# Adjacency transpositions ahead of the node tiles' stages in the hooks between passes

## The chip, the cores and the metric

The kernel runs on one core of a Trainium2 chip (trn2). Times are microseconds (us) of device time of one execution. The core has a matrix engine (TensorE, "PE", with its weight loads shown as "PEld"), a vector engine (VectorE, "DVE"), a scalar engine (ScalarE, "ACT"), GpSimd ("POOL") and a queue engine that issues DMAs (SyncE, "SP"). Each runs its own instructions in the order in which they were laid out.

## The reference

Four graph layers work on 3327 nodes with 512 features and one dense 0/1 adjacency `adj` (3327 x 3327, int32). Layers 0 to 2 are graph attention with 8, 4 and 8 heads, layer 3 is a mean over neighbours followed by a dense layer:

```python
h = jnp.maximum(_layernorm(x, axis=-1), 0.0)
# attention layer (0; layers 1 and 2 alike)
Wh = jnp.einsum('nd,hdo->hno', h, W)
e = jax.nn.leaky_relu(f1[:, :, None] + f2[:, None, :], negative_slope=0.2)   # f1, f2: Wh . a1, Wh . a2
e = jnp.where(adj[None, :, :] > 0, e, NEG_INF)
h_prime = jnp.einsum('hnm,hmo->hno', jax.nn.softmax(e, axis=-1), Wh)
x = x + elu(h_prime)
# layer 3
agg = mask @ h / jnp.maximum(deg, 1.0)
x = x + relu(concat([h @ W_self + b_self, agg @ W_nb + b_nb]) @ W_comb + b_comb)
```

## The kernel before

The nodes are cut into 26 tiles of 128 rows (the last has 127). Output rows are worked in seven *chunks*: six of four tiles and one of two. Neighbour tiles are gathered in five *groups* of 6, 6, 6, 4 and 4 tiles (`JG`).

**Attention.** For every chunk and head, the loop in `attention` builds two 0/1-like matrices per group (`tht`, `gt`: comparisons on ACT, L652, and on DVE, L649, then a bitwise "and" and "xor" with the transposed mask, L656 and L658). Then come *passes*: in layer 0 a pass is two row tiles times 26 neighbour tiles times two matmuls (L748 and L751), 104 matmuls in all, accumulated in two PSUM buffers `acc`. DVE reduces the result (L766) and later steps normalise it.

**Hooks.** After every pass `hooks.run` is called once. A hook emits a little of two other kinds of work, so that it runs between the passes:

- *Node stages.* When a chunk of layer l is done, its rows go on to layer l+1, tile by tile, one stage per hook. Every third hook takes up a new tile. Stage 0 is `finish`: load the tile's x rows (SP), two activations (L848, L849, ACT), a combination (L850, DVE), an addition on POOL (L851) and its store, issued by POOL (L852). Then follow the statistics of the normalisation (L330 and L334 on DVE, L335 to L337 on POOL), the normalised rows (L342, ACT), their transposition on PE (L138, four 128 x 128 blocks into a PSUM tile `tp`, copied out by ACT at L142), the projection (L398, 16 matmuls in layer 0's attention), scaling (L429, L432, L435), splitting into pieces (L372 on DVE, L376 and L382 on ACT, L364 and L380 on POOL) and stores (SP; also L500, a small transposition, and L503 once per chunk).
- *Mask steps.* In layer 0 the adjacency is transposed. One piece is one row tile and one group: 130 pieces. A piece is loaded by a DMA that POOL issues (L226, tile `at`, int32 to bf16, three buffers), turned by PE (L234, one 128 x 128 transposition per neighbour tile, into a PSUM tile `tp`), made into a mask by DVE (L238; for pieces on the diagonal also L241 and L242) and stored by SP (L243). Pieces at an edge first have a DVE memset (L223, L225). One mask step turns piece i-1 and then loads piece i. A hook of chunk 0 runs one or two steps in turn; a hook of a later chunk runs two in every third hook and one else. The 130 pieces end in chunk 4 of layer 0; after that the list of mask steps is empty.

Both L138 and L234, and the small transpositions, share two PSUM buffers of the name `tp`.

Before the attention of layer 0 there is a *node phase* that projects all 26 tiles of layer 0. It is a loop over the same `hooks.run`, with no pass between two hooks; from its third turn on each hook also runs one mask step (21 of them, for 20 pieces).

In layer 0's chunk 0 (layer 0 has no finished chunk yet) the hooks have no node stages, only mask steps and, from head 3 on, one of eight folds of the next layer's weights (L316 and L320, DVE).

**Order.** The framework lays out each engine's instructions; it need not keep the order in which the code emits them, but it keeps data dependences and the orders that `after` states. `after(inst, name)` puts an instruction behind another in that order, and makes no wait on the chip. The load and the first transposition of a mask step, and the first operation of most node stages, are put behind `gone[-1]`, the last matmul of the pass that has just been emitted:

```python
ld = nc.gpsimd.dma_start(at[:n, :w], adj[t * P:t * P + n, j0 * P:j0 * P + w])
after(ld, gone[-1] if gone else stored[NT - 1] if c else relus[-3])
```

The load of x rows in layer 0's `finish` stands behind the first pass only (`gone[0]`), and L848 to L852 have no such order.

Of the kernel before, what the change touches and what calls it, by code (L numbers as in the profile page):

```python
# [52 lines left out]
def tile_gnn(ctx: ExitStack, tc: tile.TileContext, x, adj, W0, a01, W1, al, ar, W2, a2,  # L53
# [197 lines left out]
    def mask_tiles(c, self_loops=False):  # L251
        t0, nt = chunks[c]
        tiles, loops = [], []
        for g, (j0, nj) in enumerate(JG):
            v = mask_view(c, g)
            nc.sync.dma_start(v, maskd[c][g])
            if self_loops:
                for k in range(nt):
                    if j0 <= t0 + k < j0 + nj:
                        loops.append((v[:, k, t0 + k - j0, :].bitcast(U32), dg1[:, t0 + k, :].bitcast(U32)))  # L260
            tiles.append(v)
        if self_loops != "later":
            set_loops(loops)
        return (tiles, loops) if self_loops == "later" else tiles
# [328 lines left out]
    class Hooks:  # L593
# [3 lines left out]
            self.masks, self.tiles, self.flying, self.small, self.done = [], [], [], [], 0  # L597

        def run(self, every, n, masks=1, steps=1):
            for st in list(self.flying):  # L600
                for _ in range(min(steps, len(st))):
                    st.pop(0)()
                if not st:
                    self.flying.remove(st)
            if self.small:
                self.small.pop(0)()
            if self.tiles and n % every == 0:
                st = self.tiles.pop(0)
                st.pop(0)()
                self.flying.append(st)  # L610
            for _ in range(masks):
                if self.masks:
                    self.masks.pop(0)()

        def drain(self):
            while self.tiles or self.flying:
# [20 lines left out]
    def matrices(L, nt, h, g, s1v, mask, pt, gt):  # L637


        l = L.l  # L640
        j0, nj = JG[g]
        gv, pv = [t[:, :nt * nj * P].rearrange("p (k j i) -> p k j i", k=nt, j=nj) for t in (gt, pt)]
        gu, pu = [t[:, :nt * nj * P].bitcast(U32) for t in (gt, pt)]
        mu = mask.rearrange("p k j i -> p (k j i)").bitcast(U32)

        def compare(jj):
            j = j0 + jj
            if j in GP_ON_DVE[l]:
                nc.vector.tensor_scalar(gv[:, :, jj, :], s1v, L.ns2[:, j, h:h + 1], 2.0,  # L649
                                        op0=ALU.is_gt, op1=ALU.mult, saturate=False)  # L650
            else:
                nc.scalar.activation(gv[:, :, jj, :], s1v, AF.Relu, bias=L.ks2[:, j, h:h + 1], scale=BIG,  # L652
                                     saturate=False)

        def split():
            nc.vector.tensor_tensor(pu, gu, mu, ALU.bitwise_and)  # L656
            if l != 1:
                nc.vector.tensor_tensor(gu, pu, mu, ALU.bitwise_xor)  # L658
        return pv, gv, (pu, mu), [lambda jj=jj: compare(jj) for jj in range(nj)] + [split]
# [219 lines left out]
    with tc.tile_pool(name="first", bufs=1) as fp:  # L879
# [30 lines left out]
        while hooks.tiles or hooks.flying:  # L910
# [4 lines left out]
            for g in range(3):  # L915
                if n == (8, 15, 21)[g]:
# [7 lines left out]
                    pv, gv, _, steps = matrices(L, PER, 0, g, early["s1"], masks0[g], b[:, :s], b[:, s:2 * s])  # L924
# [41 lines left out]
    with tc.tile_pool(name="agg", bufs=1, reuse_waits="tile") as op:  # L966
# [21 lines left out]
        for c, (t0, nt) in enumerate(chunks):  # L988
            masks = m0 if c == 0 else mask_tiles(c)
# [476 lines left out]
```

## Time and profile before

| | us |
|---|---|
| median of 3 runs | 3612.37 |
| lowest and highest | 3606.46, 3613.09 |
| the profiled execution, its own time | 3606.74 |
| its span in the profile | 3605.0 |
| first transposition L234 starts, last one ends | 37.2, 1012 |

| group of instructions | number | busy us | mean ns |
|---|---|---|---|
| L748 and L751, matmuls of the passes (PE), each | 10744 | 1838 | 249 |
| L234, transpositions of adjacency (PE) | 676 | 60.0 | 221 |
| L238, masks out of PSUM (DVE) | 110 + 20 | 91.9 + 16.9 | 844 |
| L226, loads of adjacency, issue on POOL | 130 | 73.7 | 568 |
| L851, additions of `finish` (POOL) | 72 | 124.6 | 1730 |
| L852, their stores, issue on POOL | 72 | 46.6 | 647 |
| L138, transpositions of node tiles (PE) | 416 | 64.5 | 279 |
| L142, their copies (ACT) | 108 | 62.0 | 576 |

Matmuls overlap in the array, so a mean of 249 ns goes with a distance of some 84 ns between two of them. "Idle before" and the list of waits name what an engine waited for last; idle time of an engine other than the one that bounds a stretch costs nothing. The view by stretch gives, for each stretch, its length, the busy time and number of instructions of PE, PEld, DVE, ACT and POOL, the granted share of PE's clock, the busy share of the DMA engines and GB/s.

### The profile page before, as it was taken

How to read it: one execution, taken by the hardware profiler on the slowest of the kernel's cores; microseconds unless marked ns; L12 is line 12 of the kernel's file. 1: busy time of each engine (PE TensorE's matmuls, PEld its weight loads, DVE VectorE, ACT ScalarE, POOL GpSimd, SP SyncE). 2: the span in 40 equal slices, each digit the busy share in tenths (PEclk: the TensorE clock that was granted, in tenths of full speed). 3: DMA queues.
4: the chain of work that ended last, by engine and by line, in shares of the span. 5: the costliest groups of instructions: out<-in, count | busy, mean ns of one | idle time of the engine just before them, and what ended most of it. 6: DMA issues, size and time to landing. Idle time of an engine off the chain costs nothing. (4 is left out here: it accounts for less than half of the span.)

```text
span 3605.0 us, 78609 instructions
## 1 busy us (share of the span) xinstructions
PE 3480.3 (97%) x31323; PEld 3143.9 (87%) x31323; DVE 2660.0 (74%) x5227; ACT 2512.7 (70%) x4113; POOL 633.4 (18%) x858
## 2 busy tenths in 40 slices
PE   7899999999999899999999989999999999999999
PEld 6799999999999878888888869989898989876887
DVE  8798887878887779898888868877676767672221
ACT  5777787777787888888888767766676667572111
POOL 6601221111110211232323230001010101020000
PEclk9999999999999999999999999999999999999999
DMA  7787786777766878777777876655555555576431
GB/s 219 226 239 204 205 235 195 214 206 214 223 203 205 294 261 295 263 271 280 273 255 275 296 286 214 200 168 174 179 194 178 175 177 184 166 262 250 128 97 61
DMA packets 321384, 779.00 MB, mean 216 GB/s; under 512 B 36233, under 2 KB 145108, under 8 KB 320368
## 3 DMA queue, kind: packets, MB, share of 16 engines
q1 hardware_dynamic: 287154, 704.38, 58.1%
q0 software_dynamic: 28128, 62.42, 7.4%
q10 hardware_dynamic: 5726, 7.08, 0.6%
q8 instruction: 249, 4.08, 0.4%
q14 instruction: 127, 1.04, 0.1%
HBM read 663.59 MB, written 129.64 MB: 220 GB/s over the span
## 5 line engine op out<-in xcount | busy, mean ns | idle before, releaser
L751 PE MATMUL acc<-ab,gt 128*128 128x195 bf16 (+1 forms) x10744 | 1837.8, 249 | 8.2 <-DVE rc L788 3.7
L748 PE MATMUL acc<-ab,tht 128*128 128x195 bf16 (+1 forms) x10744 | 1838.2, 249 | 6.9 <-DVE tht L656 6.0
L652 ACT ACTIVATE gt<-s1b,ks 128x512 fp8e4<-128x512 f32 (+1 forms) x2448 | 1449.8, 680 | 337.9 <-PE acc L751 204.8
L751 PEld LDWEIGHTS <-gt 128*128 128x128 fp8e4 x10744 | 1055.4, 98 | 28.6 <-issue 19.4
L748 PEld LDWEIGHTS <-tht 128*128 128x128 fp8e4 x10744 | 1055.4, 98 | 19.8 <-DVE tht L656 7.3
L656 DVE TENSOR_TENSOR tht<-gt,m 128x768 uint32<-128x768 uint32 (+3 forms) x557 | 445.4, 800 | 133.0 <-ACT gt L652 130.9
L658 DVE TENSOR_TENSOR gt<-tht,m 128x768 uint32<-128x768 uint32 (+3 forms) x557 | 449.3, 807 | 8.7
L649 DVE TENSOR_SCALAR gt<-s1b,ns 128x512 fp8e4<-128x512 f32 (+1 forms) x446 | 221.7, 501 | 161.8 <-PE acc L751 158.8
L741 PE MATMUL acc<-ab,ts 128*128 128x258 f32 x2496 | 333.4, 289 | 6.2 <-ACT ts L624 3.4
L624 ACT CAST ts<-tht 128x1536 fp32r<-128x1536 fp8e4 x208 | 300.3, 1472 | 54.6 <-PE acc L741 51.3
L741 PEld LDWEIGHTS acc<-ab,ts 128*128 128x128 f32 x2496 | 313.3, 190 | 14.7 <-issue 3.8
L1002 PE MATMUL acc<-y,mf 128*128 128x512 f32 x1352 | 311.4, 392 | 2.3 <-DVE mf L997 2.3
L652 ACT ACTIVATE tht<-s1b,ks 128x512 fp8e4<-128x512 f32 (+1 forms) x504 | 308.9, 683 | 3.3 <-DMA s1b<-s 2.8
L1002 PEld LDWEIGHTS acc<-y,mf 128*128 128x128 f32 x1352 | 254.7, 188 | 58.8 <-DVE mf L997 2.7
L766 DVE TENSOR_REDUCE R<-acc 128x130 f32<-128x390 f32 x416 | 214.8, 557 | 100.6 <-PE acc L751 99.9
L851 POOL TENSOR_TENSOR xt<-xt,e 128x512 f32<-128x512 f32 x72 | 124.6, 1730 | 913.2 <-DVE e L850 588.1
L744 PE MATMUL acc<-ab,tht 128*128 128x387 bf16 x1248 | 225.8, 329 | 7.0 <-DMA ab<-ab 3.8
L999 ACT CAST mf<-m 128x768 fp32r<-128x768 fp8e4 (+1 forms) x78 | 59.2, 763 | 247.2 <-PE acc L1002 235.4
L741 PE MATMUL acc<-ab,tv 128*128 128x258 f32 x1664 | 218.7, 283 | 0.9 <-DMA ab<-ab 0.4
L741 PEld LDWEIGHTS acc<-ab,tv 128*128 128x128 f32 x1664 | 207.1, 189 | 2.5 <-DVE tv L624 1.0
L398 PE MATMUL mm<-w,hT 128*128 128x260 f32 (+1 forms) x832 | 197.0, 391 | 8.5 <-DVE AB L435 5.1
L380 POOL TENSOR_TENSOR pt<-r 128x520 bf16<-128x520 f32 (+1 forms) x116 | 136.6, 1198 | 318.0 <-DVE r L372 301.1
(160 smaller groups left out, 3516.3 us busy)
## 6 DMA issues: line engine op xcount, KB each, us to landing
ab<-ab SPq DMA_DIRECT2D x333, 600.0 KB, 5.4
ab<-ab SPq DMA_DIRECT2D x222, 400.0 KB, 4.0
ab<-ab SPq DMA_DIRECT2D x112, 774.0 KB, 6.2
ab<-ab SPq DMA_DIRECT2D x112, 516.0 KB, 5.7
ab<-ab SPq DMA_DIRECT2D x56, 582.0 KB, 6.0
s1b<-s SPq DMA_DIRECT2D x120, 256.0 KB, 5.9
m<-mask SPq DMA_DIRECT2D x69, 384.0 KB, 4.0
ab<-pt SPq DMA_DIRECT2D x13, 1600.0 KB, 7.2
```

The lines of the kernel that those rows point to most:

```text
L398: mm = nc.tensor.matmul(pw[:, o:e], hT[:, k, :], L.w[:, k, f, o:e], start=(k == 0), stop=(k == KC - 1))
L624: (nc.scalar.copy if KIND[g] == "s" else nc.vector.tensor_copy)(t[:, :k1 - k0, :nj], th[a][g][:, k0:k1])
L649: nc.vector.tensor_scalar(gv[:, :, jj, :], s1v, L.ns2[:, j, h:h + 1], 2.0, op0=ALU.is_gt, op1=ALU.mult, saturate=False)
L652: nc.scalar.activation(gv[:, :, jj, :], s1v, AF.Relu, bias=L.ks2[:, j, h:h + 1], scale=BIG, saturate=False)
L656: nc.vector.tensor_tensor(pu, gu, mu, ALU.bitwise_and)
L658: nc.vector.tensor_tensor(gu, pu, mu, ALU.bitwise_xor)
L741: mm = nc.tensor.matmul(acc[k][:, :2 * DA], thr[g][:, k - ks[0], jj, :], ab[a][g][:, jj, :], start=(j == 0), stop=(j == NT - 1), skip_grou ...
L744: mm = nc.tensor.matmul(acc[k][:, :3 * DA], th[a][g][:, k, jj, :], ab[a][g][:, jj, :3 * DA], start=(j == 0), stop=(j == NT - 1), skip_grou ...
L748: nc.tensor.matmul(acc[k][:, :3 * DA + o], th[0][g][:, k, jj, :], ab[0][g][:, jj, :3 * DA + o], start=(j == 0), stop=False, skip_group_che ...
L751: mm = nc.tensor.matmul(acc[k][:, AO:AO + 3 * DA + o], th[1][g][:, k, jj, :], ab[0][g][:, jj, AO:AO + 3 * DA + o], start=False, stop=(j == ...
L766: nc.vector.tensor_reduce(R[:, k], v.rearrange("p a (s d) -> p a d s", s=3), AX.X, ALU.add)
L1002: nc.tensor.matmul(acc[k], mf[:, jj, :], y2[g][:, jj, s, :], start=(j0 + jj == 0 and s == 0), stop=(j0 + jj == NT - 1 and s == 1))
```

## The change

The two lines that run the mask steps move from the end of `Hooks.run` to its beginning. In every hook the mask steps are now emitted ahead of the running node tiles' stages, of the fold, and of the first stage of a new tile. Nothing else is changed; the operations, their number and their data are the same. Where a mask step looks up `gone[-1]` it finds the same matmul as before; in the node phase `relus[-3]` is read before the hook adds a tile's activation to the list, so it names that of the tile before.

```diff
         def run(self, every, n, masks=1, steps=1):
+            for _ in range(masks):
+                if self.masks:
+                    self.masks.pop(0)()
             for st in list(self.flying):
                 for _ in range(min(steps, len(st))):
                     st.pop(0)()
...
                 st = self.tiles.pop(0)
                 st.pop(0)()
                 self.flying.append(st)
-            for _ in range(masks):
-                if self.masks:
-                    self.masks.pop(0)()
```

## Prediction

> **What bounds the kernel now.** I read the page first. TensorE (PE) is busy for 97% of the span, every other engine for 74% or less, so work moved about on the others costs nothing until it makes PE wait. Adjacency is transposed only up to 1012 us (line L234 below), so only that part is affected directly; I asked for busy time by stretch: node phase of layer 0, then its row chunk 0, then its chunks 1 to 4, where the last transposition runs.
>
> ```profile
> PE 3480.3 (97%) x31323; PEld 3143.9 (87%) x31323; DVE 2660.0 (74%) x5227; ACT 2512.7 (70%) x4113; POOL 633.4 (18%) x858
> ```
> ```profile
> 0.00:160.00 160.00, 127.20 (x640) 105.63 (x641) 128.01 (x241) 103.57 (x218) 111.03 (x181) 0.94 0.75 216
> 160.00:329.00 169.00, 164.97 (x1921) 162.38 (x1920) 148.79 (x298) 132.47 (x220) 20.97 (x35) 0.98 0.80 237
> 329.00:1013.00 684.00, 653.86 (x7336) 640.44 (x7334) 555.67 (x1090) 512.76 (x865) 120.79 (x185) 0.98 0.75 212
> ```
>
> The columns are length, then busy PE, PEld, DVE, ACT, POOL. The third stretch leaves PE idle for 30.1 us. The list of waits and the view of tile `at` say on what, and how long a load takes to land:
>
> ```profile
> PE tp L234 <- DMA at<-in_adj_dram: 30.6, 11, 5.1
> ```
> ```profile
> L234 PE MATMUL tp<-identb,at x676: 216/219/314, 37.2 to 1012.1; 128*128 128x128 bf16 x169
> ...
> DMA to landing us min/median/max: 2.9/4.8/10.2
> ```
>
> Two of the 11 waits (1.1 us) are in chunk 0; nine, 29.5 us, are at hooks of chunks 1 to 4 that run two mask steps ("double hooks"): the second step transposes a tile whose load the first step issued in the same hook. One of them, on PE and on POOL:
>
> ```profile
> 394.94 0.60 PE L138 MATMUL tp<-ident,h 128*128 128x128 f32 x4
> 395.37 0.50 PE L234 MATMUL tp<-identb,at 128*128 128x128 bf16 x6
> ...
> 399.48 0.51 PE L234 MATMUL tp<-identb,at 128*128 128x128 bf16 x6 [2.18 <-DMA at<-in_adj_dram]
> ```
> ```profile
> 392.59 1.82 POOL L851 TENSOR_TENSOR xt<-xt,e 128x512 f32<-128x512 f32 x1 [14.48 <-DMA xt<-in_x_dram]
> 394.71 0.58 POOL L852 DMA_DIRECT2D x<-xt  x1 [0.30 <-POOL xt L851]
> 395.29 1.07 POOL L226 DMA_DIRECT2D at<-in_adj_dram  x2
> ```
>
> POOL works in order. A node tile's addition L851 waited 14.48 us for its x rows, and the loads of `at` stood behind it and the store L852; the load issued at 395.29 landed at 399.44 and PE stood until then. Where POOL was free the load went out far ahead and PE did not wait. A long wait also costs afterwards: after the 4.47 us wait ending at 335.52 the matmuls come 0.16 us apart instead of 0.08 until 341.1. By the length of the passes (16.6 us there, 9.2 to 9.4 in a like hook without a wait) the nine waits cost some 41 us.
>
> **What the Trainium skill says.** "DMA: Bandwidth & Descriptors", section "SWDGE vs HWDGE vs iDMA": a DMA that converts its type is issued from GpSimd alone; here all 130 loads of `at` (int32 to bf16) are POOL's. The same page, "Anatomy of one DMA", fits 2.0 us + bytes/436e3 us; 128 x 768 int32 (393 KB) gives 2.9 us, this trace's minimum, against a median of 4.8 us: the measured figures are used. "TensorE: Matmul & The Clock Gate", Part 1, has the array drop to half rate after about 3.4 us idle and need about as long to return; the trace agrees on the halving, but takes 5.3 us to return.
>
> **The change, part by part.** No instruction, wait or byte is added or removed; in each hook the mask steps are emitted ahead of the node stages. Emission is not the order of execution: the second L234 of a double hook sits inside the next pass, and at 333.07 us POOL runs L851 of a tile emitted three hooks later. The emission order acts as a priority among instructions ready together. What moves with a mask step: on POOL the load L226 (0.54 us of issue), on DVE a memset of `at` in tiles at an edge (L225, 0.06 us; L223, 0.38), L238 (0.84) and for 26 tiles the diagonal's L241 and L242 (0.59), on PE L234, on SP the store L243 (0.3).
>
> *Node phase.* Hooks follow each other with no pass between, so stages-masks-stages-masks becomes masks-stages-masks-stages: the same ring, with the 20 masks one hook (about 5 us) earlier. One transposition (PE 6 x 0.08 = 0.5 us, DVE L238 0.95 us) leaves the tail and joins the head, near 30 us, where DVE is continuously busy. Gain at most 1.5 us; cost at most the same plus one early load, 393 KB at the page's 216 GB/s = 1.8 us, among the first x rows. Between -1.5 and +3.3, taken as 0.
>
> *Chunk 0.* There are no node stages, only eight weight folds (DVE 0.69 + 0.68 us) in hooks 8 to 15, which fall behind an L238 of 0.84 us. No PE wait there hangs on either: 0, at most 1 us if a fold becomes late for layer 1; it has over 50 us.
>
> *Hooks with a projection* (one per node tile, 16). L398 takes 3.5 us and then came L234; now L234 is first, needing its `at` 3.5 us earlier. I took each tile's landing from the trace: the tightest of the 16 is the turn at 613.60, landed 609.67, 3.9 us before. Still 0.4 us in hand; cost 0, at worst 1 us. If that cover goes, PE stands with L398 behind it.
>
> *Double hooks with a node transposition* (16). L234 (0.4 to 0.5 us) now precedes L138, whose copy L142 on ACT moves back as much. The second L234 takes the PSUM buffer which L142 frees. L142 ended 0.1 us ahead of that L234 at 365.7, 0.2 ahead at 708.3 and 879.3, about 1 us ahead in most others; in the four at 431, 602, 779 and 951 ACT was late for other reasons and PE already waits 0.13 to 0.22. Moving it 0.45 costs 0.2 to 0.4 us in some three hooks: +1 us, between 0 and 4. DVE's L238 comes earlier, and L372 or L435 behind it up to 0.95 us later, one pass ahead of their need: 0.
>
> *POOL and SP.* Both loads of a hook now rank ahead of its L851 and L852. But a load is ordered behind the pass's last matmul, and L851 is not, so it can still be placed first. In all 23 double hooks from 329 us the second L234 stands 1.9 to 2.2 us behind the pass's end, before any wait, whether the run had one or not: the order was laid out with POOL free at that point, L851 and L852 already past. They were late only on the chip. So the ranking changes nothing in most; where L851 ended after the pass did (331 us, perhaps 739 and 917), L852 may fall behind the load, 0.58 + 0.30 us each. Gain 0 to 3 us, taken as 1. On SP the mask store L243 moves with its L238, ahead of node stores; x rows (SP) are ordered by free buffers: 0, within 1.
>
> The sum: +1 - 1 = 0. The profiled execution took 3606.74 us (span 3605.0 and 1.7 around it), 5.6 under the median 3612.37; on the scale of the median I predict 3612.
>
> **Rivals.** *The loads overtake (faster).* If the ranking does put the load ahead of L851 where PE waited, up to 41 us go: 3571 if in all nine, 3592 in half, 3605 if only L852 is overtaken in eight (8 x 0.88). For: POOL's order above is the cause of the waits. Against: the even 2 us, and the ordering behind the last matmul. *The PSUM buffer (slower).* If the second L234 gets the buffer of the first, freed by L238 on DVE instead of L142, it waits for L238: in the trace L238 ends after that L234's start by 0.05 to 3.0 us in 12 of the 16 double hooks with L138, 14.0 us together, and DVE, 81% busy in this stretch, evicts the pass first. Less what the earlier L234 saves, about 10 to 14: 3624. It decides where L142 is laid out later than L238. For: L142's place on ACT was already the limit in four hooks. Against: L142 ended 0.8 to 4.1 us ahead of L238 in 13 of the 16. *It does nothing:* if ties are few, the engines' order is hardly altered: 3612, on the forecast's side. A further spread comes from a layout that shifts by tenths of a us and so makes or removes a 4 to 7 us wait at another of the 23 hooks.
>
> **How the numbers follow.** 0.2% is 7.2 us, about what a measurement of this kernel can tell. No change in balance has 0.50 (its own range 3605 to 3619); slower 0.32, the buffer or two new DMA waits of 7 us, 3620 to 3630; faster 0.18, waits lost at two or more hooks, 3571 to 3604. For 8 in 10 the range takes in the buffer rival and two waits lost: 3596 to 3630.
>
> **What would show it.** Right: the first stretch stays within 3 us of 160; L234 precedes L138 and L398 on PE; nine or so waits of L234 on `at` remain, near 30 us; POOL still has L851 ahead of L226 at 395. Waits of L234 on DVE L238 mean the buffer rival; L226 ahead of L851 and PE idle in the third stretch under 15 us mean the faster one; a change after 1013 us, or in the node phase by over 5 us, means that I looked in the wrong place.

## Result and the profile after

| | before | after |
|---|---|---|
| median (us) | 3610.75 | 3611.93 |
| lowest and highest | 3600.95, 3614.79 | 3605.49, 3623.74 |
| executions | 12 | 12 |
| the profiled execution, its own time and span | 3606.74, 3605.0 | 3614.18, 3612.4 |

The ratio after to before is 1.0009, with a 95% interval from 0.9998 to 1.002. That is no change in time, and 3611.93 lies beside the predicted 3612. The profiled execution of after happens to be 7.4 us longer than that of before; executions of one and the same kernel lie up to 18 us apart, so that difference says nothing by itself. The two profiles are used here for where PE waits.

The first line is from the page of after (busy time of each engine), the next three are its view by stretch (length, busy PE, PEld, DVE, ACT, POOL, granted clock, DMA share, GB/s):

```profile
PE 3484.3 (96%) x31323; PEld 3144.2 (87%) x31323; DVE 2656.3 (74%) x5227; ACT 2510.3 (69%) x4113; POOL 622.8 (17%) x858
```
```profile
0.00:160.00 160.00, 126.15 (x643) 104.44 (x644) 124.25 (x241) 102.57 (x217) 111.44 (x181) 0.95 0.74 216
160.00:329.00 169.00, 163.75 (x1927) 161.44 (x1926) 149.34 (x298) 132.84 (x221) 21.43 (x35) 0.99 0.79 237
329.00:1013.00 684.00, 653.42 (x7308) 639.03 (x7306) 554.72 (x1087) 510.47 (x862) 120.28 (x185) 0.98 0.74 212
```

The same number of instructions runs, and in the third stretch (chunks 1 to 4) PE is busy for 653.42 us instead of 653.86. On the total alone the change does nothing. The list of waits of PE, cut to 329 to 1013 us, says otherwise (us in total, times, longest), first of before, then of after:

```profile
PE tp L234 <- DMA at<-in_adj_dram: 29.5, 9, 5.1
PE tp L234 <- ACT hT L142: 0.4, 2, 0.2
```
```profile
PE tp L234 <- DMA at<-in_adj_dram: 24.7, 9, 4.5
PE tp L138 <- DVE st L238: 3.4, 4, 1.6
PE tp L500 <- DVE st L238: 1.2, 1, 1.2
PE tp L138 <- DVE d L241: 0.8, 1, 0.8
PE tp L138 <- ACT pt L382: 0.4, 1, 0.4
```

So the load waits lost 4.8 us, and 5.8 us of another kind of wait came in: the node transpositions L138 and L500, which are not in the list of before, now wait for a PSUM buffer `tp`, which, but for 0.4 us, is DVE's to empty. **Two effects of 5 us cancel.**

The hook that the prediction showed is still as it was on POOL:

```profile
391.36 1.88 POOL L851 TENSOR_TENSOR xt<-xt,e 128x512 f32<-128x512 f32 x1 [13.80 <-DMA xt<-in_x_dram]
393.53 0.58 POOL L852 DMA_DIRECT2D x<-xt  x1 [0.30 <-POOL xt L851]
394.11 1.07 POOL L226 DMA_DIRECT2D at<-in_adj_dram  x2
```

On PE it has a new order:

```profile
393.75 0.50 PE L234 MATMUL tp<-identb,at 128*128 128x128 bf16 x6
...
399.59 0.51 PE L234 MATMUL tp<-identb,at 128*128 128x128 bf16 x6 [3.49 <-DMA at<-in_adj_dram]
400.52 0.79 PE L138 MATMUL tp<-ident,h 128*128 128x128 f32 x4
```

L851 still waits for its x rows, ahead of the load, and PE still waits for the load (3.49 us here, 2.18 before). But L138 did not land between the two L234, where the prediction had put it: it stands behind both. Here that costs nothing, because the first L234's buffer was emptied while PE stood for the load (L238 ended at 398.6). In a double hook whose load is on time it does cost. The same hook of before (first fence, PE timeline) and of after (second fence: PE, then DVE):

```profile
460.39 0.60 PE L138 MATMUL tp<-ident,h 128*128 128x128 f32 x4
460.83 0.39 PE L234 MATMUL tp<-identb,at 128*128 128x128 bf16 x4
...
462.57 0.50 PE L234 MATMUL tp<-identb,at 128*128 128x128 bf16 x6
```
```profile
462.55 0.39 PE L234 MATMUL tp<-identb,at 128*128 128x128 bf16 x4
...
464.71 0.50 PE L234 MATMUL tp<-identb,at 128*128 128x128 bf16 x6
...
466.85 0.63 PE L138 MATMUL tp<-ident,h 128*128 128x128 f32 x4 [1.56 <-DVE st L238]
```
```profile
463.94 1.23 DVE L372 TENSOR_TENSOR r<-AB 128x1032 f32<-128x1032 f32 x1
465.08 1.03 DVE L766 TENSOR_REDUCE R<-acc 128x130 f32<-128x390 f32 x2
466.03 1.54 DVE L238 TENSOR_SCALAR st<-tp 128x512 fp8e4<-128x512 bf16 x2
```

There are two `tp` buffers and three users in this hook. Before, the third user was the second L234, and the first to come free was the buffer of L138, which ACT's L142 (0.6 us) had emptied by 461.6. After, both L234 come first and the third user is L138. Both buffers are then DVE's to empty, and DVE does L372 and L766 first: L238 starts at 466.03, 3.1 us behind the end of the first L234, and L138 stands for 1.56 us.

### The profile page after: what moved, and what is told of

The parts are those of the page before. It is cut to its first block, busy times and chain, and to the rows that moved or that the text cites. A ratio compares the mean times of both kernels' runs of the same rounds, so it can differ in the third digit from the quotient of the medians.

```text
span 3612.4 us, 78611 instructions
## 1 busy us (share of the span) xinstructions
PE 3484.3 (96%) x31323; PEld 3144.2 (87%) x31323; DVE 2656.3 (74%) x5227; ACT 2510.3 (69%) x4113; POOL 622.8 (17%) x858
## 3 DMA queue, kind: packets, MB, share of 16 engines
q14 instruction: 128, 1.05, 0.1%
## 5 line engine op out<-in xcount | busy, mean ns | idle before, releaser
L748 PEld LDWEIGHTS <-tht 128*128 128x128 fp8e4 x10744 | 1054.6, 98 | 21.6 <-DVE tht L656 8.2
L766 DVE TENSOR_REDUCE R<-acc 128x130 f32<-128x390 f32 x416 | 214.7, 556 | 100.1 <-PE acc L751 99.5
L851 POOL TENSOR_TENSOR xt<-xt,e 128x512 f32<-128x512 f32 x72 | 124.0, 1722 | 920.5 <-DVE e L850 591.4
L398 PE MATMUL mm<-w,hT 128*128 128x260 f32 (+1 forms) x832 | 200.4, 395 | 10.5 <-ACT hT L142 5.4
L744 PEld LDWEIGHTS <-tht 128*128 128x128 fp8e4 x1248 | 118.0, 98 | 85.8 <-DMA ab<-ab 4.3
```

What stands on the lines that cost most here:

```text
L398: mm = nc.tensor.matmul(pw[:, o:e], hT[:, k, :], L.w[:, k, f, o:e], start=(k == 0), stop=(k == KC - 1))
L744: mm = nc.tensor.matmul(acc[k][:, :3 * DA], th[a][g][:, k, jj, :], ab[a][g][:, jj, :3 * DA], start=(j == 0), stop=(j == NT - 1), skip_grou ...
L748: nc.tensor.matmul(acc[k][:, :3 * DA + o], th[0][g][:, k, jj, :], ab[0][g][:, jj, :3 * DA + o], start=(j == 0), stop=False, skip_group_che ...
L766: nc.vector.tensor_reduce(R[:, k], v.rearrange("p a (s d) -> p a d s", s=3), AX.X, ALU.add)
```

## The experiments

All the kernels of this table were profiled. "Length" runs from the last pass of chunk 0 to the last pass of chunk 4, and "idle" is PE's idle time in it. The medians belong to separate comparisons with the kernel before (its median was 3606.37 for the first four rows, 3608.57 for the next four, 3607.58 for the next two, 3602.93 for the last two), so ratios are what to compare.

| kernel | median | ratio to before, 95% interval | idle | length |
|---|---|---|---|---|
| before_again | 3614.52 | one execution | 30.7 | 693.6 |
| after_again | 3603.78 | one execution | 30.7 | 691.4 |
| lead2_before | 3573.66 | 0.9912 (0.9896 to 0.9928) | 9.0 | 660.8 |
| lead2_after | 3593.85 | 0.9965 (0.9952 to 0.9978) | 23.1 | 678.5 |
| lead2_first_ahead | 3581.57 | 0.9932 (0.992 to 0.9945) | 14.8 | 669.7 |
| lead2_shift_before | 3562.1 | 0.9873 (0.9857 to 0.9888) | 0.0 | 649.0 |
| lead2_shift_after | 3563.31 | 0.9882 (0.9867 to 0.9897) | 0.0 | 649.3 |
| held_after | 3586.28 | 0.9944 (0.9933 to 0.9956) | 14.6 | 668.8 |
| held_before | 3585.75 | 0.9941 (0.9928 to 0.9953) | 11.1 | 665.8 |
| first_ahead | 3613.17 | 1.0015 (1.0009 to 1.0022) | 28.8 | 691.8 |
| shift_before | 3565.16 | 0.9895 (0.9877 to 0.9913) | 1.3 | 650.5 |
| shift_after | 3572.36 | 0.991 (0.989 to 0.993) | 2.1 | 652.1 |

For comparison, the first profiles have 30.1 idle and 692.5 of length (before), 30.6 and 694.7 (after).

My theory after the first two profiles: what the change really does is the new waits for `tp` buffers ("buffer theory"); the 4.8 us less of load waits might be no more than loads landing earlier or later from execution to execution. The rival was that both are effects of the change.

### The same two kernels once more

No edit: a second profile of each.

> The kernel before, unchanged, profiled once more, to see how much its waits vary from one execution to the next. Theory A (POOL's order is the same in both kernels, so the waits of L234 on the load of at do not depend on the change, and their sum of 29.5 us before against 24.7 us after in layer 0's chunks 1 to 4 is variation): the sum lies anywhere in 22 to 33 us, single waits differ by a us or two. Rival B (the change itself shortens these waits by 5 us, which pays for new waits of the node transposition): the sum is 29.5 us again within 1.5. Both: no wait of L138 or L500 on DVE's L238 after 180 us.

> The changed kernel, profiled once more. Theory A: the sum of L234's waits on the load of at in chunks 1 to 4 lies anywhere in 22 to 33 us. Rival B: 24.7 us again within 1.5. Both: L138 still stands behind the second L234 of each double hook and waits there for L238 or another late engine, 5 to 7 us in six or so hooks with L500.

Both effects came back. The nine load waits are 30.1 us in the second profile of before (4.06 of them listed there as a wait for ACT, in the same hook) and 24.95 us in that of after. The waits of L138 and L500 are 5.8 us again, term by term (3.35, 1.25, 0.79, 0.40). Variation as the reason of the 4.8 us is out: the rival holds. Most of it is one wait: the load of row tile 22's last group was issued 1.9 us ahead of its pass's end before and 3.3 us ahead after, since the L851 in front of it ran 1.4 us earlier, and it took 8.8 us to land against 5.9. So its wait went from 4.85 to 0.63 us (4.06 and 0.77 in the second profiles). SP issues a load of `ab` (L702) 2.7 us ahead of that pass's end in all four profiles; before, the load of `at` went out behind it, after, ahead of it. Whether that is why the same 262 KB landed 2.9 us sooner is not shown. The other eight waits are 24.6 us together before and 24.1 after, with single ones up to 1.3 us longer or shorter. Two of them shrank in both pairs of profiles (2.61 to 2.20 and 2.31 to 1.62 in the first): their loads went out 0.6 to 0.7 us earlier, counted from the pass's end, because L851 ended earlier. The loads still stand behind L851 and L852 there. In POOL's order of L851, L852 and L226 only two places differ between the kernels, the same two in both pairs: row tile 13's fourth load and row tile 22's second now stand ahead of an L851. Neither is one of the nine. The two profiles of one kernel differ by 8 to 10 us in span, and the second time it is before that is the longer one; chunks 1 to 4 last 692.5 and 693.6 us before, 694.7 and 691.4 after. So the 7.4 us between the first two profiles are not the change's.

### The load waits taken away: two steps of lead

A load is issued two mask steps ahead of its transposition instead of one, in both orders of emission (there are three `at` buffers).

```diff
-        return [lambda ss=[work[i - s][s] for s in (1, 0) if 0 <= i - s < len(work)]: [s() for s in ss]
-                for i in range(len(work) + 1)]
+        return [lambda ss=[work[i - 2 * s][s] for s in (1, 0) if 0 <= i - 2 * s < len(work)]: [s() for s in ss]
+                for i in range(len(work) + 2)]
```

> The kernel before with the loads of at one mask step earlier: a step turns piece i-2 and loads piece i, so no double hook turns a piece that it loads itself. Theory: the nine waits of L234 on the load (29.5 us, some 41 us with the slow matmuls after the long ones) vanish, and the time is 3560 to 3580 us, ratio 0.986 to 0.992. L138 is first in its hook, the second L234 waits for L142 at most some tenths of a us. Rival: POOL, not the length of the lead, is late, and most waits stay in other hooks: above 3595.

> The same earlier loads with the mask steps ahead of the node stages, as in the changed kernel. With the waits on loads gone the change stands alone. Theory A (PSUM buffers of the name tp are given out in the order of emission: L138 comes third in a double hook and waits for L238 of the first L234 on DVE): waits of L138 on DVE in most of 16 double hooks, 0.5 to 1.5 us each, 8 to 20 us above the kernel with stages first, so 3573 to 3595. Rival C (the plan leaves enough matmuls ahead of L138 for L238 to be done): both kernels within 4 us of each other, L138 waiting under 3 us in all.

The waits of PE from 325 to 1013 us, first of lead2_before, then of lead2_after:

```profile
PE tp L234 <- ACT hT L142: 6.4, 8, 0.8
PE tp L234 <- ACT s1t L502: 1.4, 2, 1.2
```
```profile
PE tp L138 <- DVE st L238: 12.2, 11, 2.3
PE tp L138 <- DVE d L241: 3.2, 2, 1.9
PE tp L500 <- DVE st L238: 3.1, 2, 1.8
PE tp L138 <- ACT gt L652: 2.1, 1, 2.1
PE tp L500 <- DVE d L241: 1.4, 1, 1.4
```

The load waits are gone from both (0.3 us is left in lead2_after). What remains is mostly the buffer's price: with the order of before, 8 us on ACT, in waits of up to 0.8 and 1.2 us where I had expected some tenths; with that of after, 22.7 us, of which 19.9 on DVE. The times differ by 3593.85 - 3573.66 = 20.2 us, and the intervals of the ratios lie apart. So **the change alone costs some 20 us where the load waits do not cover it**. In idle time that is 23.1 - 9.0 = 14.1 us, against 5.2 in the kernel as it was, because there L238 is done while PE stands for the load: in after none of the nine hooks with a load wait has a wait of L138 or L500, in lead2_after eight of the same nine have one, 12.8 us together.

### Only the first step ahead

One mask step is emitted ahead of the node stages and the other behind them, so that PE's order becomes L234, L138, second L234. That is the order which my prediction had reckoned with.

```diff
         def run(self, every, n, masks=1, steps=1):
+            if masks and self.masks:
+                self.masks.pop(0)()
             for st in list(self.flying):
...
-            for _ in range(masks):
+            for _ in range(masks - 1):
```

Two readings of how `tp` buffers are given out were set against each other here: in turn, as in a ring, or whichever comes free first, as from a pool.

> Earlier loads, and in each hook the first mask step ahead of the node stages, the second behind them: in a double hook L234, L138, L234, the order on which the prediction reckoned. Ring theory (the two PSUM buffers go round in the order of emission): the second L234 waits for L238 of the first on DVE, 0.5 to 2 us in most of the 16 double hooks with L138, 3583 to 3595. Pool theory (whoever is next takes the buffer that comes free first, here L138's by L142): no waits on L238, at most the tenths on L142, 3568 to 3578, like the kernel with earlier loads and stages first.

> Only the first mask step of a hook is emitted ahead of the node stages, the second one stays behind them: on PE the order L234, L138, second L234 that the prediction assumed. Buffer theory (L138's waits of the kernel after come from the third tp buffer in order of emission): no wait of L138 on L238 in chunks 1 to 4, waits of L234 on L142 or L502 of 0.5 to 4 us, those on the DMA 24 to 31 us: ratio to the kernel before 0.999 to 1.001. Rival, that the earlier first L234 costs by itself: waits of L138 on L238 stay at 3 us or more.

Waits of PE from 325 to 1013 us, lead2_first_ahead and then first_ahead:

```profile
PE tp L234 <- ACT s1t L502: 6.7, 3, 2.9
PE tp L234 <- ACT hT L142: 4.8, 6, 0.8
PE tp L234 <- DMA at<-in_adj_dram: 1.8, 2, 1.3
PE tp L234 <- DVE st L238: 1.5, 2, 1.3
```
```profile
PE tp L234 <- DMA at<-in_adj_dram: 27.5, 11, 4.7
PE tp L234 <- ACT hT L142: 0.9, 3, 0.4
```

With L138 second, no L138 waits for L238, with or without the lead. The third user, the second L234, waits for a copy by ACT, nearly always: it gets the buffer that comes free first, as the pool reading has it. The waits for L142 tell the two readings apart, since in a ring this L234 would follow the first one and wait for L238 (1.5 us here). That settles the cause of the waits of after: L138's place behind both L234. The time alone would not have told it: the measured 3581.57 lay nearer to what I gave for the ring than to what I gave for the pool. L502, the copy of the small transposition at a chunk's start, is what I had left out, with 6.7 us against 1.4 in lead2_before.

first_ahead has 1.3 us less idle and 0.7 us less length than before, but a median 5.6 us above that of before, at a ratio of 1.0015, where I had expected 0.999 to 1.001. Its profiled execution, with 3607.43 us, is one of its fastest and shows no cause for that. It stays open, below the 0.2% that I had set as what can be told.

### No node transposition in the double hooks

The hooks with two mask steps move to those hooks in which no stage uses a `tp` buffer and no L851 is emitted. This was done with two steps of lead and without.

```diff
-                        hooks.run(1 if last else 3, hook, 2 if hook % 2 and c == 0 or hook % 3 == 0 and c else 1, 2 if last else 1)
+                        hooks.run(1 if last else 3, hook, 2 if hook % 2 and c == 0 or hook % 3 == 2 and c else 1, 2 if last else 1)
```

> Earlier loads, stages first, and the double hooks moved from every third hook that also has L138 (hook mod 3 = 0) to the one after the projection (hook mod 3 = 2), where no node transposition uses a PSUM buffer of the name tp. The waits of the second L234 on L142 (8 x 0.8 us) vanish: 3564 to 3572. If something else than L142 bounds those hooks: 3574 as with earlier loads alone.

> The same with the mask steps ahead of the stages. Buffer theory (the change costs time only where three users of two tp buffers meet in one hook): L138 now has at most one L234 ahead of it, no waits on L238 of over 1 us in all, and the time is within 5 us of the kernel with stages first, where with the double hooks at mod 3 = 0 the change cost some 20 us. Rival (the change costs through DVE's order, L238 ahead of L372, L435 and L418 in every hook): still 10 us or more above the kernel with stages first.

> Only the hooks with two mask steps move, from hook % 3 == 0, where a new tile's L851 is emitted, to hook % 3 == 2, where no stage uses a tp buffer; a load is still issued by the step before its transposition. If what makes the loads late is the L851 emitted in the same hook, the waits of L234 on the DMA fall under 10 us in chunks 1 to 4: 3565 to 3585. Rival: the load of a double hook is issued at the pass's end in any case and lands 3 to 5 us later, against a place 2 us behind it: 16 double hooks or more wait 1 to 3 us, 3590 to 3610.

> The same with the order of emission of the kernel after. As no stage of these hooks uses a tp buffer, buffer theory expects no wait of L138 on L238 and the time of the previous kernel within 4 us; if it is 5 us or more above that, the change costs in another way than by the buffers.

The stretch from 329 to 1013 us, first of lead2_shift_before, then of lead2_shift_after:

```profile
329.00:1013.00 684.00, 683.98 (x7841) 674.60 (x7840) 596.40 (x1169) 551.12 (x933) 128.98 (x194) 1.00 0.77 226
```
```profile
329.00:1013.00 684.00, 684.00 (x7815) 674.47 (x7813) 595.08 (x1167) 551.91 (x933) 128.87 (x192) 1.00 0.77 226
```

PE is idle for 0.02 us in 684, and the order of emission makes no difference: 3562.1 and 3563.31 with overlapping intervals. **The change costs only where L138 or L500 shares a hook with two L234**; the rival, a cost through DVE's order in every hook, fell. (3562.1 lies a little below the 3564 to 3572 expected.) Without the lead it is nearly as good: 1.3 us idle, and a load wait only in shift_after (0.8 us in two). So the lateness of the loads was tied to the hook in which they were asked for: one where a new tile's L851 is emitted. The rival of shift_before, loads that are 1 to 3 us late in any hook, fell. shift_after is 7.2 us above shift_before, which is over the 4 us expected and over the 5 us from which I had said that the change costs in another way too, though the intervals overlap. Its profiled execution is 12.8 us longer than that of shift_before; 1.6 us of that lies in chunks 1 to 4 and 8.4 us ahead of them. The end of chunk 0 scatters over 10 us among all these kernels: 315.9 to 323.8 in the six with the order of before, mean 320.0, and 315.6 to 325.7 in the six of after, mean 319.6. So 8.4 us lies within that scatter, and with two steps of lead the same pair lies the other way round (320.9 and 315.6). That the 7.2 us between two medians of four executions is scatter as well is likely, but not shown.

lead2_shift_before beats both kernels, by 1.3%; the shift alone is worth 1.05% (0.9895), and the intervals of the two overlap, so what the lead adds is not settled. (In the four kernels with shifted hooks the last transpositions fall into chunk 5, so their lengths are a little short.)

### L851 held back

L851 of layer 0's hooks is put behind the pass's last matmul in the planned order, as the loads are, so that it can't be planned earlier than they. Again with both orders of emission.

```diff
-        nc.gpsimd.tensor_add(xt, xt, e)
+        ad = nc.gpsimd.tensor_add(xt, xt, e)
+        if l == 0:
+            after(ad, gone[-1])
```

> The changed kernel with L851 of layer 0 ordered behind the last matmul of its pass, as the loads of at already are: now POOL's loads, ranked first, do overtake L851 and L852. This is the prediction's faster rival made true. If those two are what delays the loads: the waits of L234 on the load fall from 25 us to under 8, L138's waits on L238 grow to about 12 (there is less time for L238 behind a wait), 3580 to 3598. If the loads are late for other reasons: the waits stay over 18 us and the time within 5 us of the changed kernel.

> Order of emission as in the kernel before; only L851 of layer 0's hooks is put behind the pass's last matmul in the planned order, as the loads of adjacency already are. Theory that the ranking decides ties (the change is needed for the loads to pass L851): L851 and L852 are emitted first, so they stay ahead of L226 on POOL in most double hooks, and waits of L234 on the DMA stay at 20 to 32 us in chunks 1 to 4: 3600 to 3612. Rival, holding L851 is enough without the change: DMA waits under 8 us and, with no L138 waiting for L238, 3570 to 3585.

POOL of held_before ahead of a double hook, whose pass ends at 363.5 (L854 is the store, L852 before the edit). L851, L854 and the second L226 are emitted in this hook; that L226 loads what it turns last:

```profile
351.21 0.62 POOL L226 DMA_DIRECT2D at<-in_adj_dram  x1
351.86 1.40 POOL L851 TENSOR_TENSOR xt<-xt,e 128x512 f32<-128x512 f32 x1
353.21 0.57 POOL L226 DMA_DIRECT2D at<-in_adj_dram  x1
353.77 0.55 POOL L854 DMA_DIRECT2D x<-xt  x1
```

The waits of PE from 329 to 1013 us in held_before, then in held_after:

```profile
PE tp L234 <- DMA at<-in_adj_dram: 10.5, 3, 4.3
```
```profile
PE tp L138 <- DVE st L238: 6.2, 7, 1.6
PE tp L234 <- DMA at<-in_adj_dram: 3.1, 1, 3.1
PE tp L138 <- DVE d L241: 2.2, 2, 1.4
PE tp L500 <- DVE d L241: 1.4, 1, 1.4
PE tp L500 <- DVE st L238: 1.3, 1, 1.3
```

I had expected of held_before that the order of emission decides among instructions held to the same matmul, so that L851 would stay ahead of the loads without the change, with 20 to 32 us of load waits. L851 does stay ahead of its own hook's load, as above, but the waits that should follow did not come. L851 no longer waits on POOL for x rows (no such wait from 325 to 1013 us, 76.2 us in before), because it is no longer laid out up to three hooks ahead of the one that emits it. The load above went out 10.3 us ahead of its pass's end, the same load in before 5.8 us ahead, and six of the nine load waits are gone with the old order already. So that theory fell; the bounds of its rival (under 8 us of load waits, at most 3585) were just missed. The gain of 22 us comes from L851's place in the plan, not from the ranking. The change adds to it what it does everywhere: two further load waits go, at the first hooks of chunks 1 and 3, where L851 still stood first on POOL in held_before (10.5 to 3.1 us in all), and 11.5 us of waits for buffers come in. The idle time is 14.6 us against 11.1, and the times do not tell the two apart: 3586.28 and 3585.75.

## Why the prediction was right, and where it was not

- **What bounds the kernel.** Right. PE's waits behind late loads were worth what I took from the lengths of the passes: 41 us estimated; 38 us gained without them (3602.93 - 3565.16, shift_before), 46 with the lead as well (3608.57 - 3562.1).
- **POOL: -1, between -3 and 0.** Right in mechanism. L851 stays ahead of L226, since it was laid out earlier than the load, and held_before and held_after show that this place is the reason. What I had said of L852 did not come true: at 331, 739 and 917 us it still stands ahead of the load. The term was mis-sized, too: the load waits fell by 4.8 us, more than the 3 allowed, and 4.2 of it at the one load that went out 1.4 us earlier and landed 2.9 us sooner, the latter for a reason still open.
- **Node phase: 0, between -1.5 and +3.3.** Right: PE is idle for 33.8 us up to 160 us in after and 32.9 in its second profile, 32.8 and 33.5 in those of before. The first transposition moved from 37.2 to 27.5 us, near the 30 that I had given.
- **Chunk 0: 0, at most 1.** PE's idle time from 160 to 329 us went from 4.0 and 4.4 us to 5.3 and 5.2. It is the 1 us that was the upper bound.
- **Hooks with a projection: 0.** Right. L234 precedes L398 in all 16, and these hooks' passes are 12.5 to 12.8 us long in after, 12.5 to 12.6 before. The hook that I had called the tightest had no time in hand: its L234 started as the load landed (616.3), some 0.2 us late; in the second profile the load was 0.1 us ahead.
- **Double hooks: +1, between 0 and 4.** This is the step that failed. I reckoned with L234, L138, second L234, and with a second L234 that waits for L142. Both mask steps of a hook are emitted ahead of L138, so both are planned ahead of it, and the one that waits is L138, for DVE's L238. The term measured 5.8 us, less the 0.64 that L234 had waited for L142 before (0.4 in the list of waits, which leaves out the smallest): +5.2 us.
- **The sum** was right by cancelling, which is luck: -4.8 and +5.2 where I had -1 and +1, both outside their ranges, and PE's idle time from 325 to 1025 us went from 30.1 to 30.6.
- **The rivals.** The buffer rival was right about the buffer, DVE's lateness and the size of its uncovered price (14.0 us counted from the trace of before; the extra idle time with the lead is 23.1 - 9.0 = 14.1), but named the wrong instruction, and I did not see that its price is hidden where the same hook waits for a load. That cover, and the 4.8 us, are why slower did not happen: without load waits the change costs 20 us. The faster rival needed loads that pass L851. The change itself brings that about at two loads that PE did not wait for; with L851 held as well, it does so at most double hooks. "It does nothing" is refuted by the waits, though its time is the same.

## To carry to other kernels

Where a pair of PSUM buffers serves three users in one stretch, ask who is third in order of emission and which engine empties the buffers of the first two; do not leave the user whose buffer is emptied fast (0.6 us on ACT here) for the third place. With the loads out early, L138 first took 3573.66 us, second 3581.57 and third 3593.85. Better than any of these was to keep the three out of the same hook (3562.1). A time that does not move is no proof that nothing happened: list the waits by cause before and after, and remove the one that covers the other. Where an engine works in order, look for what was planned ahead of the late instruction before you change the priorities behind it.

## What was not expected of the hardware

Loads of adjacency land after 2.8 to 9.1 us in after (median 5.2), for at most 393 KB; the prediction's fit by the Trainium skill, "DMA: Bandwidth & Descriptors", section "Anatomy of one DMA", gave 2.9 us for such a load. None was that fast: the minimum of 2.9 us in before, which the prediction set beside it, belongs to a load of 262 KB, and the fastest of 393 KB took 3.3 us.

A wait cost more than its length. Taking the 30.1 us of idle time out of chunks 1 to 4 (lead2_shift_before) shortened them by 43.5 us (692.5 to 649.0) and the kernel by 46. The clock granted to PE accounts for most of the rest: in before it is at half for 23.9 us of these chunks, in five spells of 3.4 or 6.8 us, each at a load wait, and in lead2_shift_before it is never reduced there. Half the speed for 23.9 us costs some 12 us, by this estimate. The prediction gave the halving some 3.4 us of idle time; in before the clock fell for 3.4 us at a wait of 2.61 us (569.0), and in before_again it did not at one of 3.39 us (402.4), so the length of the wait alone does not decide it here.
